# Attention projections by seven block products instead of eight, with the block sums on GpSimd and VectorE

## Chip, core and metric

One core of a Trainium2 chip runs the whole program. The metric is the device time of one execution in microseconds (us); the times shown are of separate runs, and beside them stands one execution recorded by the hardware profiler. Engines: PE is TensorE (matrix products; PEld its weight loads), DVE is VectorE, ACT is ScalarE, POOL is GpSimd, SP is the engine that issues most DMA transfers. On-chip memory is SBUF (128 partitions); matrix products are written to PSUM, which has eight banks. All data here are fp32.

## The reference, cut to what matters

1250 nodes with 768 features pass through two graph-attention layers, then through a transformer block: multi-head attention with 12 heads of 64, and a mixture of experts (8 experts, 2 per token). Only the attention's projections are changed:

```python
def _attention(x, Wqkv, Wproj):
    B, T, D = x.shape                      # 1, 1250, 768
    qkv = (x @ Wqkv).reshape(B, T, 3, H, HD)
    q, k, v = (qkv[:, :, 0], qkv[:, :, 1], qkv[:, :, 2])
    scores = jnp.einsum('bqhd,bkhd->bhqk', q, k) * jnp.float32(HD) ** (-0.5)
    attn = jax.nn.softmax(scores, axis=-1)
    out = jnp.einsum('bhqk,bkhd->bqhd', attn, v).reshape(B, T, D)
    return out @ Wproj
```

## The kernel before, in words

The input of attention is `yT`: the normalized rows, transposed, 128 partitions x 6 chunks of features (`DC`) x 1250 nodes. It is filled tile by tile (ten tiles of 125 nodes, `NT`) by the second graph layer: aggregation matmuls `pagg` (L524), layernorm on VectorE (L120 to L134), six transposes `ptr` on PE (L141) and six activations on ScalarE that write `yT` (L147).

Attention works on two heads at a time (`p`, six pairs) and on a third of the queries at a time (`CHUNKS`, 417 or 416 columns), so there are 18 units (`class Unit`). A unit's scores are computed while the unit before it is being finished. For each of ten key tiles, `scores` multiplies keys by queries into `st`, ScalarE copies `st` to `sT` (L679) and VectorE keeps a running maximum `most` (L685). Then `top` transposes `most` (`ptop`, L692), VectorE reduces it to `m` (L694), `row` spreads `m` over partitions into the PSUM tile `mb` (L701), `weights` subtracts it (L706, VectorE), takes the exponential (L707, ScalarE) and adds up the weights (`acc`, L712, GpSimd), and `values` multiplies by the values (`pav`, L720). `divide` of the unit before sums `acc` over partitions on PE (`pz`, L729) and divides on VectorE (L735, L736), writing `aT`.

Queries and keys of a pair of heads come from `queries_keys` (L639), a generator: each `yield` ends one step, and `go` runs steps at chosen places inside the three units of the pair before. Its steps are single matmuls: 2 and 4 in a unit's head, around `top` and `divide`, and three times 2 in the loop over key tiles. Keys are written to a PSUM tile with the tag of `mb` and queries to one with the tag of `pz`; ScalarE moves them out (L642). The values come from `value_rows` (L655), per tile of 125 nodes 12 matmuls into a pair of banks from `pair_psum`, moved out by ScalarE (L658).

What sets the order: inside `manual_schedule` PE runs exactly in the written order. The other engines' instructions are ordered by the framework's list scheduler when the program is built; each engine's queue then runs strictly in that order, and semaphores make one engine wait for another. A pool of tiles that takes memory of an earlier pool waits for all of that pool; with `reuse_waits="tile"` it waits only for the tiles that lay there. With `bufs=1` a tile waits until its predecessor under the same tag has been read.

From the program as it is built: `pagg` has PSUM banks 0 to 3 and `ptr` banks 4 to 6; in attention `pair_psum` has banks 0 to 3, the tag `mb` banks 4 and 5, `pz` bank 6, `pav` bank 7. In SBUF `cnt`, the graph's edge counts, lies where `aT` lies later.

Of the kernel before, what the change touches and what calls it, by code (L numbers as in the profile page):

```python
# [10 lines left out]
F32 = mybir.dt.float32  # L11
# [16 lines left out]
def gnn_ffn_kernel(  # L28
# [569 lines left out]
                transpose_rows(gpt, y, affine(yT, t, 0))  # L598


    attn = late.enter_context(tc.tile_pool(name="attn", bufs=1))
    aT = attn.tile([P, DC, N], F32, name="aT")
    with tc.tile_pool(name="att", bufs=2) as ap, \
            tc.tile_pool(name="aps", bufs=2, space=PSUM) as aps, \
            tc.tile_pool(name="apm", bufs=1, space=PSUM) as apm, \
            tc.tile_pool(name="apa", bufs=1, space=PSUM) as apa:
        heads = [slice(i * HD, (i + 1) * HD) for i in range(2)]
        BW = 105
        NB = 4
# [3 lines left out]
            return aps.tile([P, 2, 512], F32, tag="s", name=name)  # L613


        zero = ap.tile([P, RW], F32, name="zero", bufs=1)
        nc.gpsimd.memset(zero, 0.0)  # L617
        nc.gpsimd.memset(zero[:, D:D + 1], float(NOWHERE))
        for e in range(NE):
# [1 line left out]
                                zero[:, None, :].to_broadcast([P, REG // P, RW]))  # L621
        nc.gpsimd.dma_start(xd[NOWHERE:NOWHERE + P, :], zero)

        def queries_keys(p):

            wqk = ap.tile([P, DC, 2, P], F32, tag="wqk", name="wqk", bufs=1)
            for i in (1, 0):
                nc.sync.dma_start(wqk[:, :, i, :], Wqkv[:, i * D + p * P:i * D + (p + 1) * P].rearrange(
                    "(c p) f -> p c f", p=P))
            qk = ap.tile([P, 2, N], F32, tag="qk", name="qk")  # L630
            yield qk
            for c0, w in CHUNKS:
                for i in (1, 0):
                    if i == 1:
                        pq = apm.tile([P, 2, 512], F32, tag="mb", name="pk")[:, 0, :]
                    else:
                        pq = apa.tile([P, 512], F32, tag="pz", name="pq")
                    for c in range(DC):
                        nc.tensor.matmul(pq[:, :w], wqk[:, c, i, :], yT[:, c, c0:c0 + w],  # L639
                                         start=(c == 0), stop=(c == DC - 1))  # L640
                        if c == DC - 1:
                            nc.scalar.mul(qk[:, i, c0:c0 + w], pq[:, :w], 1.0 if i == 1 else HD ** -0.5)  # L642
                        yield None

        def go(steps, n):
            for _ in range(n if steps is not None else 0):
# [1 line left out]

        v = big.tile([T, NT, D], F32, tag="B", name="v")

        def value_rows(t):
            pv = pair_psum("pv")
            for s in range(2):
                for c in range(DC):
                    nc.tensor.matmul(pv[:T, s, :DH], yT[:, c, t * T:(t + 1) * T],  # L655
                                     wv[:, c, s * DH:(s + 1) * DH],
                                     start=(c == 0), stop=(c == DC - 1))
            nc.scalar.copy(v[:, t, :].rearrange("p (s d) -> p s d", s=2), pv[:T, :, :DH])  # L658

        onesf = ap.tile([T, HD], F32, name="onesf", bufs=1)  # L660
        nc.vector.memset(onesf, 1.0)

        class Unit:


            def __init__(self, p, k, qk):
                self.p, self.qk = p, qk
                self.c0, self.w = CHUNKS[k]
                self.starts = [min(b * BW, self.w - BW) for b in range(NB)]
                self.s = []  # L670

            def scores(self, j):
                w = self.w
                st = pair_psum("st")
                for i, r in enumerate(heads):
                    nc.tensor.matmul(st[:T, i, :w], self.qk[r, 1, j * T:(j + 1) * T],  # L676
                                     self.qk[r, 0, self.c0:self.c0 + w], start=True, stop=True)
                s = ap.tile([T, 2, CW], F32, tag="sT", name="sT", bufs=15)
                nc.scalar.copy(s[:, :, :w], st[:T, :, :w])  # L679
                self.s.append(s)  # L680
                if j == 1:
                    self.most = ap.tile([T, 2, CW], F32, tag="most", name="most")
                if j > 0:
                    prev = self.s[0] if j == 1 else self.most
                    nc.vector.tensor_tensor(self.most[:, :, :w], prev[:, :, :w], st[:T, :, :w], ALU.max)  # L685
# [18 lines left out]
            def weights(self, j):  # L704
                w, s = self.w, self.s[j]
                nc.vector.tensor_tensor(s[:, :, :w], s[:, :, :w], self.mb[:T, :, :w], ALU.subtract)  # L706
                nc.scalar.activation(s[:, :, :w], s[:, :, :w], AF.Exp)  # L707
                if j == 1:
                    self.acc = ap.tile([T, 2, CW], F32, tag="acc", name="acc")
                if 0 < j < self.ns:  # L710
                    prev = self.s[0] if j == 1 else self.acc
                    nc.gpsimd.tensor_tensor(self.acc[:, :, :w], prev[:, :, :w], s[:, :, :w], ALU.add)  # L712
# [22 lines left out]
                nc.vector.reciprocal(rz[:, :w], self.pz[:, :w])  # L735
                nc.vector.tensor_tensor(aT[:, self.p, self.c0:self.c0 + w], self.pav[:, :w], rz[:, :w], ALU.mult)  # L736

        steps = queries_keys(0)
        qks = [next(steps)]
        wp = load_big_weight(Wproj, "wp")  # L740
        BEFORE = 2
        with tc.manual_schedule(engines={mybir.EngineType.PE}):
            for t in range(BEFORE):
                value_rows(t)
            for _ in steps:
                pass
            u = Unit(0, 0, qks[0])
            for j in range(NT):
                u.scores(j)
                if j + BEFORE < NT:  # L750
                    value_rows(j + BEFORE)
        units = [(p, k) for p in range(DC) for k in range(NCK)]
        steps = last = None
        for n, (p, k) in enumerate(units):
            if k == 0:
                steps = None
                if p + 1 < DC:
                    steps = queries_keys(p + 1)
                    qks.append(next(steps))
            nxt = Unit(*units[n + 1], qks[units[n + 1][0]]) if n + 1 < len(units) else None  # L760
            u.ns = NT if nxt is not None else NS
            with tc.manual_schedule(engines={mybir.EngineType.PE}):

                go(steps, 2)
                u.top()
                if last is not None:
                    last.divide()
                go(steps, DC - 2)
                if nxt is not None:
                    nxt.scores(0)  # L770
                u.row()
                u.weights(0)
                u.weights(1)
                for j in range(0, NT, 2):
                    for i in range(2):
                        if nxt is not None and j + i > 0:
                            nxt.scores(j + i)
                    if j < 6:
                        go(steps, 2)
                    for i in range(2):  # L780
                        if j + i + 2 < NT:
                            u.weights(j + i + 2)
                    for i in range(2):
                        u.values(j + i)
            last, u = u, nxt
# [306 lines left out]
```

## Time and profile before

| | |
|---|---|
| median of 3 runs | 1527.41 us (1524.62 to 1529.33) |
| profiled execution | 1522.34 us, span 1520.5 us |
| granted PE clock over the span | 0.963 |
| PE busy | 1433.7 us (94%) |
| DVE busy | 811.9 us (53%) |
| ACT busy | 595.6 us (39%) |
| POOL busy | 418.6 us (28%) |
| values (`pv`, L655) | 240 matmul instructions, 79.9 us busy |
| queries and keys (`pq`, `pk`, L639) | 432 matmul instructions, 172.1 us busy |

How to read the lines that follow: a timeline line has the start in us from the beginning of the span, the length in us, engine, source line, operation, output<-inputs with their shapes, the count of merged instructions, and in brackets how long the engine stood idle before it and what released it. A group line has busy time and mean length (ns) of one. The page's section 2 cuts the span into 40 slices of 38 us; each digit is a busy share in tenths. Values and the first queries and keys are computed from about 555 to 670 us, the units run from about 670 to 1160.

### The profile page before, as it was taken

To read this page: it belongs to the slowest core of one execution; us is meant where nothing else is said; L and a number is where in the kernel's file an instruction comes from. 1 tells how busy PE (TensorE), PEld (TensorE's weight loads), DVE (VectorE), ACT (ScalarE), POOL (GpSimd) and SP (SyncE) were. 2 spreads that over 40 slices of the span, in tenths; PEclk is the share of its full clock that TensorE was granted. 3 is DMA by queue.
4 is the path that set the end of the run, shared out by engine and by line. 5 is a ranking of instruction groups with operands and counts; after the bars stand their busy time and mean duration, and the time that the engine had idled before them with its cause. 6 is when DMAs were issued, how large, how long until landed. Compare 5 with 4: busy or idle time off the path is not lost.

```text
span 1520.5 us, 15858 instructions
## 1 busy us (share of the span) xinstructions
PE 1433.7 (94%) x5952; PEld 779.0 (51%) x5952; DVE 811.9 (53%) x1311; ACT 595.6 (39%) x924; POOL 418.6 (28%) x276
## 2 busy tenths in 40 slices
PE   6787999999999999999999999999989996899997
PEld 4574555556555555543343343344333664565654
DVE  6688456434036640127778778778787764111111
ACT  4221513205116521136556646646656354221211
POOL 5000000000000010006646646655657222122222
PEclk9758999999999999999999999999999997899999
DMA  7000020010021139920000000000120432855643
GB/s 207 22 2 11 11 73 0 0 32 1 15 88 45 57 100 396 407 86 0 22 1 0 22 1 21 1 22 0 28 75 1 144 119 107 300 172 185 219 153 134
DMA packets 48199, 124.66 MB, mean 82 GB/s; under 512 B 5629, under 2 KB 22207, under 8 KB 48120
## 3 DMA queue, kind: packets, MB, share of 16 engines
q1 hardware_dynamic: 31468, 57.36, 11.5%
q0 software_dynamic: 11968, 56.26, 9.8%
q10 hardware_dynamic: 4684, 9.99, 2.2%
q8 instruction: 48, 0.79, 0.2%
q14 instruction: 31, 0.25, 0.1%
HBM read 70.47 MB, written 57.60 MB: 84 GB/s over the span
## 4 chain that ended last, share of the span: by engine, by line
PE 67%; DVE 9%; issue 7%; ACT 4%; DMA 4%; POOL 1%; POOLq 0%; SPq 0%; ACTq 0%; DVEq 0%
PE pagg L524 13%; PE st L676 8%; PE ph L204 7%; PE pav L720 7%; PE pk L639 5%; PE pv L655 5%; PE phe L1006 5%; PE poe L1015 5%; PE pq L639 4%; DMA xd<-yn,slot 2%; DVE sT L706 2%; PE po L864 2%; ACT sT L679 1%; DVE most L685 1%; PE mb L701 1%
## 5 line engine op out<-in xcount | busy, mean ns | idle before, releaser
L712 POOL TENSOR_TENSOR acc<-acc,sT 125x834 f32<-125x834 f32 (+1 forms) x139 | 273.1, 1964 | 10.9
L524 PE MATMUL pagg<-h,wt 125*125 125x385 f32 (+1 forms) x800 | 263.5, 486 | 0.4 <-DVE wt L517 0.4
L685 DVE TENSOR_TENSOR most<-most,st 125x834 f32<-125x834 f32 (+1 forms) x144 | 147.0, 1021 | 105.5 <-ACT sT L679 102.6
L524 PEld LDWEIGHTS pagg<-h,wt 125*125 125x125 f32 x800 | 147.0, 187 | 104.7 <-DVE wt L517 3.5
L706 DVE TENSOR_TENSOR sT<-sT,mb 125x834 f32<-125x834 f32 (+1 forms) x180 | 174.1, 1015 | 22.6 <-PE mb L701 22.6
L707 ACT ACTIVATE sT<-sT 125x834 f32<-125x834 f32 (+1 forms) x180 | 158.4, 900 | 49.2 <-DVE sT L706 48.8
L679 ACT COPY sT<-st 125x834 f32<-125x834 f32 (+1 forms) x180 | 151.6, 848 | 52.4 <-PE st L676 50.7
L676 PE MATMUL st<-qk 64*125 64x417 f32 (+1 forms) x720 | 164.5, 556 | 3.9 <-DVE most L685 3.8
L720 PE MATMUL pav<-sT,v 125*64 125x417 f32 (+1 forms) x720 | 151.0, 532 | 9.0 <-ACT sT L707 9.0
L617 POOL MEMSET zero<- 128x772 f32 x1 | 0.7, 742 | 530.2 <-PE ptr L141 530.2
L712 POOL TENSOR_TENSOR acc<-sT 125x834 f32<-125x834 f32 (+1 forms) x18 | 35.4, 1965 | 274.6 <-ACT sT L707 274.6
L676 PEld LDWEIGHTS st<-qk 64*125 64x125 f32 x720 | 56.5, 184 | 99.1 <-issue 42.7
L720 PEld LDWEIGHTS pav<-sT,v 125*64 125x64 f32 x720 | 42.5, 136 | 105.7 <-issue 43.9
L1015 PE MATMUL poe<-we,hT 128*128 128x384 f32 x264 | 88.8, 486 | 0.0
L639 PE MATMUL pq<-yT,wqk 128*128 128x417 f32 (+1 forms) x216 | 88.1, 534 | 0.0
L864 PE MATMUL po<-wp,aT 128*125 128x384 f32 x240 | 87.5, 498 | 0.0
L1019 DVE SCALAR_TENSOR_TENSOR sofar<-poe,weight,sofar 128x768 f32<-128x768 f32 x25 | 25.4, 1018 | 114.6 <-PE poe L1015 107.7
L1006 PE MATMUL phe<-xT,we 128*128 128x384 f32 (+1 forms) x288 | 86.6, 460 | 0.0
L639 PE MATMUL pk<-yT,wqk 128*128 128x417 f32 (+1 forms) x216 | 84.0, 526 | 0.0
L204 PE MATMUL ph<-gw,xnT 128*125 128x384 f32 x240 | 81.4, 498 | 0.5 <-DMA gw<-in_L_gnn_W_dram 0.5
L655 PE MATMUL pv<-wv,yT 128*125 128x384 f32 x240 | 79.9, 490 | 1.4 <-issue 1.4
L528 DVE RECIPROCAL rz<-pagg 125x1 f32<-125x1 f32 x20 | 3.3, 166 | 141.5 <-PE pagg L524 141.5
(222 smaller groups left out, 1788.2 us busy)
## 6 DMA issues: line engine op xcount, KB each, us to landing
xd<-zero POOLq DMA_DIRECT2D x8, 3860.0 KB, 15.2
we<-in_L_ffn_W_dram SPq DMA_DIRECT2D x16, 1152.0 KB
xr<-xd SPq DMA_DIRECT2D x25, 386.0 KB
gw<-in_L_gnn_W_dram SPq DMA_DIRECT2D x2, 2304.0 KB
wqk<-in_L_ffn_Wqkv_dram SPq DMA_DIRECT2D x12, 384.0 KB
xres<-in_x_dram SPq DMA_DIRECT2D x10, 375.0 KB
xsd<-xres ACTq DMA_DIRECT2D x10, 375.0 KB
xn<-in_x_dram SPq DMA_DIRECT2D x9, 336.0 KB
```

Source lines behind the costliest of these rows:

```text
L204: nc.tensor.matmul(po[:, s, :DH], xT[:, c, t * T:(t + 1) * T], w[:, c, s * DH:(s + 1) * DH], start=(c == 0), stop=(c == DC - 1))
L524: nc.tensor.matmul(po[:, s, :DH + s], ws[j][:, (d - d0) * T:(d - d0 + 1) * T], h[:, j, s * DH:(s + 1) * DH + s], start=(j == 0), stop=(j = ...
L639: nc.tensor.matmul(pq[:, :w], wqk[:, c, i, :], yT[:, c, c0:c0 + w], start=(c == 0), stop=(c == DC - 1))
L676: nc.tensor.matmul(st[:T, i, :w], self.qk[r, 1, j * T:(j + 1) * T], self.qk[r, 0, self.c0:self.c0 + w], start=True, stop=True)
L679: nc.scalar.copy(s[:, :, :w], st[:T, :, :w])
L685: nc.vector.tensor_tensor(self.most[:, :, :w], prev[:, :, :w], st[:T, :, :w], ALU.max)
L706: nc.vector.tensor_tensor(s[:, :, :w], s[:, :, :w], self.mb[:T, :, :w], ALU.subtract)
L707: nc.scalar.activation(s[:, :, :w], s[:, :, :w], AF.Exp)
L712: nc.gpsimd.tensor_tensor(self.acc[:, :, :w], prev[:, :, :w], s[:, :, :w], ALU.add)
L720: nc.tensor.matmul(self.pav[r, :w], v[:, j, hd0:hd0 + HD], s[:, i, :w], start=(j == 0), stop=(j == NT - 1))
L1006: nc.tensor.matmul(ph[:, :n * P], w1[:, c, f * P:(f + 1) * P], xT[:, c, :n * P], start=(c == 0), stop=(c == DC - 1))
L1015: nc.tensor.matmul(po[:, d, :DH], hT[:, f, s * P:(s + 1) * P], w2[:, f, d * DH:(d + 1) * DH], start=(f == 0), stop=(f == FC - 1))
```

## The change

A product of two matrices cut into quarters takes eight products of quarters, or seven if sums and differences of quarters are multiplied (the Strassen-Winograd form). The change uses seven for the values and for queries and keys.

- `left_sums` makes four sums of quarters of the weights and `right_sums` four of `yT`, all on GpSimd; some overwrite quarters in place, others go to `aT`, which is still unused then (`spare`), and to the tiles `t2`, `t3`, `t4`.
- `seven` runs the products, each three matmuls long. Product 1 is copied out by ScalarE; the others are added to earlier partial sums by VectorE, straight from PSUM (seven adds for six products). Products go to the banks of `mb` (`m`, `n`), `pz` (`z`) and `pav` (`v`).
- Values: the products pair tile `t` with tile `t + 5`, 384 columns wide. Queries and keys: both come from the same seven products (weights' columns: keys, queries; nodes: first half, second half), in two pieces of 313 and 312 columns. A step of `queries_keys` is now a whole product; `go` runs one before `top`, one after `divide` and three in the loop.
- The queries' scale moves into the exponential. `wp` is loaded in the last pair of heads, since its memory now holds copies of `t2` and `t3` (`kept`) till then. The scores' 15 buffers become 15 tags, `most` and `acc` get one buffer each, and the pools of attention use `reuse_waits="tile"`.

```diff
-    attn = late.enter_context(tc.tile_pool(name="attn", bufs=1))
+    attn = late.enter_context(tc.tile_pool(name="attn", bufs=1, reuse_waits="tile"))
...
-    with tc.tile_pool(name="att", bufs=2) as ap, \
+    with tc.tile_pool(name="att", bufs=2, reuse_waits="tile") as ap, \
...
-        zero = ap.tile([P, RW], F32, name="zero", bufs=1)
+        spare = aT.rearrange("p c n -> p (c n)")
+        zero = spare[:, 4 * N:4 * N + RW]
...
+        def left_sums(a, w, flat):
+            s1, s2, s4 = parts(flat, w, 3)
+            a11, a12, a21, a22 = (a[:, c:c + KH, f:f + w] for f in (0, w) for c in (0, KH))
+            nc.gpsimd.tensor_tensor(s1, a21, a22, ALU.add)
+            nc.gpsimd.tensor_tensor(s2, s1, a11, ALU.subtract)
+            nc.gpsimd.tensor_tensor(s4, a12, s2, ALU.subtract)
+            nc.gpsimd.tensor_tensor(a21, a11, a21, ALU.subtract)
+            return [a11, a12, s4, a22, s1, s2, a21]
...
+        def right(t2, t3):
+            return [y11, y21, y22, t4, y12, t2, t3]
+        def right_sums(t, t2, t3):
+            q = slice(t * T, (t + 1) * T)
+            nc.gpsimd.tensor_tensor(t3[:, :, q], y22[:, :, q], y12[:, :, q], ALU.subtract)
+            nc.gpsimd.tensor_tensor(y12[:, :, q], y12[:, :, q], y11[:, :, q], ALU.subtract)
+            nc.gpsimd.tensor_tensor(t2[:, :, q], y22[:, :, q], y12[:, :, q], ALU.subtract)
+            nc.gpsimd.tensor_tensor(t4[:, :, q], y21[:, :, q], t2[:, :, q], ALU.subtract)
+
+        FREE = ["1m", "6n", "2z", "7v", "5m", "4n", "3z"]
+        BOUND = ["1m", "6n", "7z", "4z", "2z", "5m", "3n", "1z", "6z", "7z", "4m", "2n", "5z", "3z"]
+
+        def seven(order, operands, np_, w, o11, o12, o21, o22):
...
+            for i, name in order:
+                if name == "m":
+                    two = apm.tile([P, 2, 512], F32, tag="mb", name="mq")
+                if name in "mn":
+                    b = two[:np_, "mn".index(name), :w]
+                else:
+                    b = apa.tile([P, 512], F32, tag={"z": "pz", "v": "pav"}[name], name="q")[:np_, :w]
+                for c in range(KH):
+                    lhs, rhs = operands(int(i) - 1, c)
+                    nc.tensor.matmul(b, lhs, rhs, start=(c == 0), stop=(c == KH - 1))
+                if i == "5":
+                    u4 = part(1)
+                if i == "1":
+                    nc.scalar.copy(p1, b)
+                for o, u in {"2": [(o11, p1)], "6": [(u2, p1)], "7": [(u3, u2)], "4": [(o21, u3)],
+                             "5": [(u4, u2), (o22, u3)], "3": [(o12, u4)]}.get(i, []):
+                    nc.vector.tensor_tensor(o, b, u, ALU.add)
+                yield None
...
-                nc.scalar.activation(s[:, :, :w], s[:, :, :w], AF.Exp)
+                nc.scalar.activation(s[:, :, :w], s[:, :, :w], AF.Exp, scale=HD ** -0.5)
...
+            ws = left_sums(wv, DH, spare)
+            for t in range(NU):
+                right_sums(t, t2, t3)
+            steps = queries_keys(0, right(t2, t3), True)
...
+            kept = wpool.tile([P, DC, D], F32, tag="w", name="kept").rearrange("p c d -> p (c d)")
+            ys = right(*parts(kept, NH, 2))
+            nc.gpsimd.tensor_copy(ys[5], t2)
+            nc.gpsimd.tensor_copy(ys[6], t3)
...
-                go(steps, 2)
+                go(steps, 1)
                 u.top()
                 if last is not None:
                     last.divide()
-                go(steps, DC - 2)
+                go(steps, 1)
...
                     if j < 6:
-                        go(steps, 2)
+                        go(steps, 1)
```

## The prediction

> **What bounds the kernel now.** I read the engine totals and the 40 slices first, then the groups of instructions (for the prices), then the timeline of one unit of attention, of the units that have no projection in them, and of the passage from the second graph layer into attention.
>
> ```profile
> PE 1433.7 (94%) x5952; PEld 779.0 (51%) x5952; DVE 811.9 (53%) x1311; ACT 595.6 (39%) x924; POOL 418.6 (28%) x276
> ...
> PE   6787999999999999999999999999989996899997
> ...
> DVE  6688456434036640127778778778787764111111
> ```
>
> TensorE (PE) is near full from the fourth slice on, which by itself promises a gain for every matmul taken out. But VectorE (DVE) stands at 7 to 8 all through attention (slices 18 to 30). How near to the bound that is shows in units with and without projection matmuls. In the timeline of PE, the maxima's transposes (`ptop`) mark a unit's start:
>
> ```profile
> 759.78 1.02 PE L692 MATMUL ptop<-ident,most 125*105 125x125 f32 x8
> ...
> 788.72 1.02 PE L692 MATMUL ptop<-ident,most 125*105 125x125 f32 x8
> ```
> ```profile
> 1106.10 1.10 PE L692 MATMUL ptop<-ident,most 125*105 125x125 f32 x8 [0.72 <-DVE most L685]
> ...
> 1131.82 1.10 PE L692 MATMUL ptop<-ident,most 125*105 125x125 f32 x8 [0.52 <-DVE most L685]
> ```
>
> A unit with projection takes 28.94 us, one without 25.72. The 24 matmul instructions of 0.350 us (8.4 us) that the first has and the second lacks cost only 3.2 us: just under them lies a chain of VectorE and ScalarE. The same unit on VectorE:
>
> ```profile
> 760.84 1.20 DVE L694 TENSOR_REDUCE m<-ptop 105x8 f32<-105x1000 f32 x1 [1.83 <-PE ptop L692]
> 761.95 2.75 DVE L735 RECIPROCAL rz<-pz 128x416 f32<-128x416 f32 x1
> 764.74 0.59 DVE L736 TENSOR_TENSOR aT<-pav,rz 128x416 f32<-128x416 f32 x1
> 766.70 2.89 DVE L706 TENSOR_TENSOR sT<-sT,mb 125x834 f32<-125x834 f32 x3 [1.37 <-PE mb L701]
> ...
> 778.84 1.02 DVE L685 TENSOR_TENSOR most<-most,st 125x834 f32<-125x834 f32 x1
> 780.31 1.02 DVE L685 TENSOR_TENSOR most<-most,st 125x834 f32<-125x834 f32 x1 [0.45 <-ACT sT L679]
> ```
>
> Reduce, reciprocal and multiplication follow without a gap up to 765.33; PE's transposes `mb` begin at 765.48, and from 766.70 to 779.86 VectorE has no gap. PE and VectorE are nearly even here.
>
> **Matmuls taken out, up to the first unit.** Each fp32 matmul stands in the trace as two instructions. Values: 240 become 5 pairs x 7 products x 3 x 2 = 210; 30 of them in a row took 9.84 us (from 562.47, 0.328 each): **-9.8**. First queries and keys: 72 of 417 columns at 0.350 (12 from 576.35 to 580.55) become 84 of 313. A 128-column one took 0.116 (36 `phe` in 4.18); on the line between, 313 columns take 0.266: 22.3 for 25.2, **-2.9**. VectorE adds 35 sums of 384 columns and 14 of 313 here. Price: 834 columns took 1.016 (L706), 417 took 0.591 (L736), so by the line through both 313 take 0.485 and 384 take 0.557, each under a product of 1.6 to 2.0 us, on an engine that is 0 to 2 tenths busy in these slices. Costed at nothing: the next product in the same bank comes at least two products later. Without that cover it would wait for the sum.
>
> **The passage.** Here the tail of the graph layer was filled:
>
> ```profile
> 555.51 6.04 PE L655 MATMUL pv<-wv,yT 128*125 128x384 f32 x18 [1.36 <-issue]
> ...
> 561.80 0.83 PE L141 MATMUL ptr<-ident,y 125*128 125x125 f32 x6 [0.25 <-DVE y L134]
> 562.35 2.19 ACT L147 ACTIVATE yT<-ptr,lnp 128x125 f32<-128x125 f32 x6 [1.61 <-PE ptr L141]
> ...
> 562.47 2.75 PE L655 MATMUL pv<-wv,yT 128*125 128x384 f32 x8
> 562.71 0.98 SPq L628 DMA_DIRECT2D wqk<-in_L_ffn_Wqkv_dram  x2
> ...
> 562.75 0.74 POOL L617 MEMSET zero<- 128x772 f32 x1 [530.17 <-PE ptr L141]
> ```
>
> The value rows could start at 555.51 because `pair_psum` has the banks of `pagg`, read by then. The new products write `mb`, `pz` and `pav`; these have the banks of the transposes `ptr`, which ScalarE reads until 564.54. The first of the seven waits for that, and behind it on PE, which runs this block in written order, every other product and the scores. By 564.6 the kernel before had done 18 value instructions and 6.6 more, 24.6 x 0.328: **+8.1**. The gap (554.2 to 561.8) also costs clock. Before L720 at 1112.96 PE stood idle 2.07 us; the window after it, whose last three numbers are granted clock, DMA share and GB/s:
>
> ```profile
> 1113.00:1117.00 4.00, 3.94 (x12) 1.14 (x14) 4.00 (x5) 2.56 (x3) 2.51 (x2) 0.57 0.08 25
> ```
>
> Eight `pav` took 3.08 us there where others took 1.62, the next eight `st` 2.02 for 1.67: 1.8 lost, **+1.8**. The last six transposes come after that gap; at half clock six took 1.51 (1276.94) instead of 0.83: **+0.7**.
>
> GpSimd's sums go by its row of 834 columns, 1.965: in proportion or with the slope between 834 and 832 columns (4 ns), 2.7 for each of the four of `wv` (1152 columns), 0.9 to 1.1 for each of 20 of `yT` (375), 31 in all. Tile-wise reuse lets them start when `cnt`, which lay where `aT` will, was last read (521.5, L517); with nine DMA issues of `xd` ahead (7.7 of issue, 7.8 of wait) they end near 569, but the first value products need only the first eight (near 554): hidden, by the last aggregations and then by 14 us of value products. If that cover is gone, see the third rival. The load of `wqk` can leave SP earlier than 562.71; that of `wp` moves past those of `wqk`, to the last pair of heads, some 75 us before its use: nothing. Two copies into `kept` (at most 4.4 each by the sums' rate) begin when product 4 has read `wv`; the first lies under products 3, 1 and the transposes (2.0 + 1.7 + 0.95 = 4.6), the second is needed 6 us later: nothing.
>
> A rule of the Trainium skill speaks against sums there. VectorE's maxima took 1,024 ns with GpSimd idle (600 to 672) and 1,020 with it busy (742 to 758), but those, like the new adds, have one operand in PSUM. "SBUF — State Buffer", section "SBUF: two separate sides", says that GpSimd and a VectorE instruction with two SBUF inputs or in a two-port mode lock each other out for a whole instruction; the last layernorm has such ones (L589, L134 twice), so by the rule the sum would be 1 to 3 us higher. No row shows it.
>
> **The fifteen units with projection.** A step is now one product, six instructions of 0.266 = 1.60, with 0.1 to 0.2 for the change of operands (four of 0.350 took 1.50 from 758.28, 1.60 from 767.42). A unit's head on PE, from 758.28 to `mb` at 765.48, shrinks from 7.20 to 6.20 (first step 1.70 for 1.50, second 1.80 for 3.00, transposes, row sums and first scores 2.70 as before). In the loop 8 steps of 1.80 replace 9 of 1.60 per three units: no gain. So PE offers 1.0 per unit, all of it ahead of `mb`. VectorE gets 14 adds per three units, 2.26 us per unit. Three of them (products 5 and 4 in a first step) fall into its wait for `ptop` (1.83): free. Three (6, 3 and 2 in a second step) must be done before `mb` takes the same bank. Such an add queues behind reciprocal and multiplication, which are ready first: 7.05 + 0.20 (`ptop` later) + 0.485 + 0.1 (signal, as from `mb` to L706) = 7.8 for 7.20, **+0.6**; behind it wait PE's `mb`, then all subtractions and exponentials. Ahead of the multiplication it would cost 0, ahead of the reciprocal +0.9. The loop's 8 adds (1.3 per unit) enter the stretch without gaps; scores wait on maxima there, but the last subtractions (776.04) ran some 6 us ahead of the `pav` that need them (785.66), so they can give way: +0.1, of 0 to 1.3. I take **+0.7 x 15 = +10.5**, ends -1.0 and +2.2 (-15 and +33).
>
> **GpSimd in the heads.**
>
> ```profile
> 782.57 6.05 POOL L712 TENSOR_TENSOR acc<-acc,sT 125x834 f32<-125x834 f32 x3
> ```
> Its chain of sums ends at 788.62, 1.4 after the unit's start at 787.21; PE's row sums `pz` use it at 789.66: slack 1.04, and 0.20 more with the longer first step. Four weight sums (384 columns, 1.0 each) are new per pair of heads. Behind the chain the two that product 6 needs end at 1.4 + 2.0 = 3.4, in time for it (3.5). Inside the chain they delay `pz` by 4.0 - 1.2 = 2.8. Four such heads, 0 to 11; I take 1.0 each, near the lower end, since a part can run in GpSimd's idle 10.6 us before the chain: **+4**.
>
> **Sum.** -12.7 + 10.6 + 10.5 + 4.0 = +12.4. The profiled execution took 1522.3 (span 1520.5), which gives 1534.7. The median of the runs shown is 5.1 above it: **1540**.
>
> **Rivals.** (1) Faster: the add is issued ahead of the multiplication, or VectorE's gaps take all adds, and heads shrink with PE: -12.7 + 10.6 - 0.5 x 15 to -1.0 x 15 = -10 to -17, about 1514. It decides below +0.1 per unit with GpSimd free. For it: 2.8 us of VectorE gaps at a unit's end, and 1.37 before `mb`. Against: the reciprocal's chain, and 25.72 + 2.26 = 28.0, already near 28.94. 0.20. (2) It evens out (units +0.1, GpSimd 0): 1527. 0.15. (3) Memory is not free before the last transposes: GpSimd starts at 562.75 as before, issues 7.7, sums 10.9 + 4.0: value products begin some 22 (with the ninth DMA's wait 30) us later: 1560. The memset's wait speaks for it, the tile-wise reuse against. 0.08. (4) Every add and sum lands on the path: units +1.8, GpSimd 11: +36, 1563. 0.12. My forecast, slower by 5 to 20: 0.45. That a 313-column product saves nothing is excluded by the 0.116 row.
>
> 0.3% (4.6 us) is about what a measurement can tell. Faster 0.20, same 0.15, slower 0.65. 1517 to 1560 leaves out half of (1) and most of (4).
>
> **What would show it.** PE idle of 7 us or more before the first value product, at a granted clock near 0.5 after it; 714 `q` and `mq` instructions; units of 29.3 to 30.2 between `ptop`, with the `u2` add behind `aT` and `mb` waiting on it; `pz` waiting on `acc` in the 4th, 7th, 10th and 13th unit. Units below 28.5, or value products before 562, would prove me wrong.

## The result and the profile after

The change makes the kernel slower: 1561.01 us median of 4 runs (1557.99 to 1565.51) against 1526.01 of 4 runs of the kernel before beside them (1521.51 to 1529.33), ratio 1.0229, interval 1.0210 to 1.0247. The profiled execution took 1563.34 us, with a span of 1561.6. Engine totals and slices of the changed kernel (the last line is the granted TensorE clock):

```profile
PE 1415.8 (91%) x5994; PEld 791.7 (51%) x5994; DVE 877.4 (56%) x1430; ACT 577.1 (37%) x895; POOL 471.0 (30%) x326
...
PE   5787999999999938999999999999988997799997
...
PEclk9758999999999968999999999999999998899999
```

PE is busy 17.9 us less than before, yet the span is 41.1 longer. Two slices (546 to 624 us) show 3 and 8 tenths of PE and 6 and 8 tenths of clock, where before there were nines. So most of the loss lies between the graph layer and attention, not in the units.

Two rulers split it. From the residual add of tile 6 (L589) to the first unit's top transposition (`ptop`): 158.92 us before, 191.17 after, **+32.3**. From the first `ptop` to the last (17 units): 484.89 and 489.27, **+4.4**. Together 36.6, near the 35.0 between the medians. The forecast had -2.1 and +14.5. The ends of both rulers, before:

```profile
513.70 0.95 DVE L589 TENSOR_TENSOR xres<-xres,o 125x768 f32<-125x768 f32 x1
...
672.62 1.10 PE L692 MATMUL ptop<-ident,most 125*105 125x125 f32 x8 [0.58 <-DVE most L685]
...
1157.51 1.10 PE L692 MATMUL ptop<-ident,most 125*105 125x125 f32 x8 [0.52 <-DVE most L685]
```

and in the changed kernel:

```profile
517.14 0.95 DVE L589 TENSOR_TENSOR xres<-xres,o 125x768 f32<-125x768 f32 x1
...
708.31 1.02 PE L756 MATMUL ptop<-ident,most 125*105 125x125 f32 x8
...
1197.58 1.10 PE L756 MATMUL ptop<-ident,most 125*105 125x125 f32 x8 [0.52 <-DVE most L749]
```

The passage in the timeline of the changed kernel:

```profile
543.01 0.56 POOL L624 DMA_DIRECT2D xd<-aT  x1 [6.23 <-DMA xd<-aT]
...
543.58 2.65 POOL L641 TENSOR_TENSOR aT<-aT,wv 128x1152 f32<-128x1152 f32 x1
...
544.58 15.15 DVE L589 TENSOR_TENSOR xres<-xres,o 125x768 f32<-125x768 f32 x1
...
558.07 0.84 POOL L655 TENSOR_TENSOR t<-yT 128x375 f32<-128x375 f32 x1
...
565.13 1.48 PE L141 MATMUL ptr<-ident,y 125*128 125x125 f32 x6 [14.74 <-DVE y L134]
...
566.40 8.08 PE L524 MATMUL pagg<-h,wt 125*125 125x385 f32 x18
...
574.56 61.60 SPq L697 DMA_DIRECT2D wqk<-in_L_ffn_Wqkv_dram  x4
...
582.14 1.49 PE L141 MATMUL ptr<-ident,y 125*128 125x125 f32 x6 [7.66 <-DVE onesf L720]
...
585.28 4.20 PE L680 MATMUL mq<-wv,yT 128*125 128x384 f32 x6 [1.65 <-ACT yT L147]
...
601.52 2.17 PE L680 MATMUL mq<-wv,t 128*125 128x384 f32 x6 [1.21 <-DVE v L687]
...
608.14 0.99 POOL L640 TENSOR_TENSOR aT<-wqk 128x384 f32<-128x384 f32 x1 [22.00 <-DMA wqk<-in_L_ffn_Wqkv_dram]
...
610.95 2.91 PE L680 MATMUL mq<-t,aT 128*128 128x313 f32 x6 [3.74 <-POOL aT L641]
```

Four things. VectorE's add of tile 8, 0.96 us for other tiles, lasts 15.15 and ends (559.73) 0.8 us after a train of GpSimd sums has run dry (558.91). TensorE idles 14.74 us for it and then works at half clock: 18 `pagg` in 8.08 us, 5.99 before. The first value product comes at 585.28, after the last transposes, as the forecast said. And the weights `wqk`, issued at 574.56 (the first two of the four issues that this line merges), are there only at 608.

The waits of TensorE in the changed kernel, in columns of total us, times and longest us:

```profile
PE mb L765 <- DVE qk L687: 7.8, 10, 0.8
...
PE pz L793 <- POOL acc L776: 5.7, 5, 1.3
...
PE mq L680 <- DVE v L687: 3.9, 5, 1.2
PE mq L680 <- POOL aT L641: 3.7, 1, 3.7
...
PE mq L680 <- ACT u L684: 2.5, 4, 0.7
PE mb L765 <- DVE u L687: 2.1, 4, 0.5
```

The rows `mq <- v` and `mq <- u` (and one like them, `mq <- qk`, 1.9 in all) belong to the start: product 4 (second half of the tile `mb`) waits for VectorE's adds of product 5 (first half), product 6 for ScalarE's copy of product 1. The head of a unit, from `ptop` to `mb`, in the timeline:

```profile
736.61 1.02 PE L756 MATMUL ptop<-ident,most 125*105 125x125 f32 x8
...
738.78 2.76 DVE L799 RECIPROCAL rz<-pz 128x417 f32<-128x417 f32 x1
...
741.46 0.42 DVE L687 TENSOR_TENSOR qk<-mq,u 128x313 f32<-128x313 f32 x1
...
741.79 0.58 DVE L800 TENSOR_TENSOR aT<-pav,rz 128x417 f32<-128x417 f32 x1
...
741.93 1.12 PE L765 MATMUL mb<-ident,m 105*125 105x105 f32 x8 [0.78 <-DVE qk L687]
```

The add stands behind the reciprocal but ahead of the multiplication, and `mb` follows at 5.32 us after `ptop` (5.70 before). Most units with projection last 30.2, 29.1 and 28.6 us in turn; before, nearly all of them lasted 28.9.

### The profile page after: what moved, and what is told of

It is laid out like the page before. It is cut to its first block, busy times and chain, and to the rows that moved or that the text cites. A ratio compares the mean times of both kernels' runs of the same rounds, so it can differ in the third digit from the quotient of the medians.

```text
span 1561.6 us, 16121 instructions
## 1 busy us (share of the span) xinstructions
PE 1415.8 (91%) x5994; PEld 791.7 (51%) x5994; DVE 877.4 (56%) x1430; ACT 577.1 (37%) x895; POOL 471.0 (30%) x326
## 4 chain that ended last, share of the span: by engine, by line
PE 55%; DVE 13%; issue 9%; ACT 5%; POOL 5%; DMA 4%; POOLq 0%; ACTq 0%; SPq 0%; DVEq 0%
PE pagg L524 12%; PE ph L204 7%; PE st L739 5%; PE pav L784 5%; PE mq L680 5%; PE phe L1082 5%; PE poe L1091 4%; PE q L680 4%; POOL acc L776 4%; DVE sT L770 2%; DVE rz L799 2%; DMA xd<-yn,slot 2%; ACT sT L743 2%; ACT sT L771 2%; DVE most L749 2%
## 5 line engine op out<-in xcount | busy, mean ns | idle before, releaser
L770 DVE TENSOR_TENSOR sT<-sT,mb 125x834 f32<-125x834 f32 (+1 forms) x180 | 174.8, 1014 | 12.7 <-PE mb L765 12.7
L204 PE MATMUL ph<-gw,x1T 128*125 128x384 f32 x240 | 78.8, 489 | 0.0
L1084 ACT ACTIVATE hT<-phe 128x384 f32<-128x384 f32 (+1 forms) x27 | 12.6, 466 | 160.4 <-PE phe L1082 157.0
L1082 PEld LDWEIGHTS phe<-xT,we 128*128 128x128 f32 x288 | 52.1, 190 | 33.7
```

The lines of the kernel that those rows point to most:

```text
L204: nc.tensor.matmul(po[:, s, :DH], xT[:, c, t * T:(t + 1) * T], w[:, c, s * DH:(s + 1) * DH], start=(c == 0), stop=(c == DC - 1))
L1082: nc.tensor.matmul(ph[:, :n * P], w1[:, c, f * P:(f + 1) * P], xT[:, c, :n * P], start=(c == 0), stop=(c == DC - 1))
```

## The experiments

All ratios are to the kernel before, run beside. "Passage" is the first ruler, "units" the second, both in us of the profiled execution. The kernels that are not in the table (e1, e6, e7, e10, e12, e14, e15) were run once each.

| kernel | median | ratio, 95% interval | passage | units |
|---|---|---|---|---|
| before | 1526 | 1 | 158.9 | 484.9 |
| changed | 1561.0 | 1.0229 [1.0210, 1.0247] | 191.2 | 489.3 |
| e2 sums on VectorE | 1556.7 | 1.0194 [1.0177, 1.0211] | 187.8 | 488.8 |
| e3 zero writes partly later | 1552.1 | 1.0177 [1.0158, 1.0195] | 179.5 | 489.8 |
| e4 own banks | 1555.2 | 1.0184 [1.0167, 1.0201] | 181.5 | 490.0 |
| e5 GpSimd's order | 1559.5 | 1.0216 [1.0196, 1.0237] | 191.3 | 484.0 |
| e8 zero writes late | 1544.1 | 1.0117 [1.0090, 1.0143] | 172.5 | 489.4 |
| e9 as e8, but sums of `wv` and `yT` on VectorE | 1545.2 | 1.0130 [1.0103, 1.0157] | 171.8 | 489.3 |
| e11 all of it | 1519.5 | 0.9958 [0.9943, 0.9972] | 151.0 | 488.1 |
| e11b sums on GpSimd | 1517.6 | 0.9937 [0.9922, 0.9953] | 148.9 | 486.9 |
| e13 two value groups first | 1518.3 | 0.9941 [0.9922, 0.9960] | 148.9 | 486.1 |

**Three trains of GpSimd work in the kernel before.** My first theory: GpSimd's train of sums locks VectorE out until it ends.

```diff
+                if t == 7:                       # behind the residual add, scratch tile dum
+                    nc.gpsimd.tensor_copy(dum[:T], xr[:, :384])
+                    for i in range(18):
+                        nc.gpsimd.tensor_tensor(dum, dum, dum, ALU.subtract)
```

> The kernel before, with 18 extra GpSimd subtractions (two SBUF inputs, 384 numbers a partition, some 0.9 us each, 16 us together) that start when tile 7's residual add is done; they work on a scratch tile, and nothing waits for them. Theory of the lock (GpSimd's train of SBUF sums keeps VectorE's two-SBUF-input add out until the train has run dry): the residual add of tile 8, some 6 us after the train's start, lasts about 10 us in place of 0.96, and ends within a microsecond of the train's end; the end of the run comes 5 to 12 us later than before's. Theory of the transfer (the add of 15.15 us in the changed kernel waited for its tile of x, slowed by the early zero writes): all ten adds stay at 0.9 to 1.0 us, and the time stays within 3 us of before's.

> The same place, with 36 GpSimd copies of 192 numbers (one SBUF input) in place of the subtractions, 8 to 14 us together. If any GpSimd instruction on SBUF keeps the add out: the add of tile 8 lasts until the train's end, 3 to 8 us. If only two-input instructions do: all adds stay at 0.9 to 1.0 us. Theory of the transfer: they stay there too.

> The same place, with 12 pairs of a subtraction (0.9 us) and a GpSimd memset (0.3 us). If the lock is held by one instruction at a time, or is freed by an instruction that reads nothing: the add of tile 8 lasts at most 1 us longer than 0.96. If GpSimd keeps it as long as it has anything queued: some 9 us, to the train's end. Theory of the transfer: 0.9 to 1.0.

The add of tile 8 took 1.55, 1.12 and 0.96 us; the times were 1527.39, 1523.59 and 1523.57 beside 1524.03. The theory in this form fell. In that train each sum read what the one before had written, so I tried one without such gaps:

```diff
+                        nc.gpsimd.tensor_tensor(m[:, (i % 2) * 384:(i % 2 + 1) * 384],
+                                                m[:, 768:1152], m[:, 768:1152], ALU.subtract)
```

> The kernel before, again with 18 GpSimd subtractions of 125x384 (two SBUF inputs) after tile 7's residual add; now neighbours write two different places of a dead tile and none reads what its neighbour wrote, so each can begin as the one before it ends, where the first train's each read the one before and stood 0.06 us apart. Theory of the lock held over a train without gaps: VectorE's residual add of tile 8, or another of its SBUF-to-SBUF steps, falls into the train and lasts until its end, 5 to 10 us, and the end of the run comes 4 to 10 us later than before's. Rival (the lock passes at every instruction's end; the 15.15 us had another cause): no VectorE step is longer than its usual time by more than 1 us, and the time is within 3 us of before's.

The add took 1.07 us, and the longest GpSimd sum 1.54 in place of 0.82: the two engines took turns. The rival held; 1528.54 us, inside the usual scatter.

**The start's sums on VectorE.**

```diff
-            nc.gpsimd.tensor_tensor(...)          # left_sums(wv), right_sums, first left_sums(wqk)
+            nc.vector.tensor_tensor(...)
```

> The changed kernel with the sums of the start (of the value weights, of the LN output, of the first head pair's weights) on VectorE in place of GpSimd; the units' sums stay on GpSimd. Theory of the lock: the residual add of the last tile is back at 1 us, its transposes come 13 to 17 us earlier, and the time falls to 1545 to 1549 us, less 2 to 4 us for the half clock that follows the idle stretch, plus up to 5 us where VectorE's own 12 us of sums delay the last tiles. Theory of the transfer: the add of the last tile stays at 15 us and the time within 3 us of the changed kernel's.

Timeline of this kernel:

```profile
545.12 0.96 DVE L589 TENSOR_TENSOR xres<-xres,o 125x768 f32<-125x768 f32 x1
...
568.73 0.96 DVE L589 TENSOR_TENSOR xres<-xres,o 125x768 f32<-125x768 f32 x1 [9.32 <-DMA xres<-in_x_dram]
```

The add of tile 8 is back at 0.96 us, but that of tile 9 now waits for its load until 568.73: a second delay had been hidden behind the first. So the time fell by some 4 us, not by the 12 to 16 of the lock theory.

**The zero writes later.** In the change GpSimd issues eight of the nine writes that fill the expert buffer `xd` (31 MB) from 529 us on, 35 us earlier than before (564), and the ninth at 543.

```diff
-        (zero and the nine writes of xd ahead of left_sums(wv))
+        (the same behind the copies into kept)
```

> The changed kernel with the zero writes of the expert buffer (31 MB, GpSimd's DMA queue) issued after the copies at the start's end in place of ahead of the sums. Theory of the transfer for the add of 15.15 us: it falls to 1 us and the time by 14 to 18 us. Theory of the lock: it stays at some 15 us (GpSimd's train starts up to 14 us earlier without the wait for the writes ahead of it, so the train may lie elsewhere and the add be shorter, but it still ends with a GpSimd instruction). Theory of the late weight load: the first head pair's weights land some 10 us earlier, the wait of 3.74 us ahead of the queries' second product goes, and with it half clock of 1.8 us: 4 to 6 us less.

Only six of the nine moved: three were still issued at 535, since nothing ties a write to its place. Directly behind those three came GpSimd's sums, and now another VectorE step lasted: the scaling `y` of L134, 5.51 us for 0.67:

```profile
535.14 2.98 POOL L817 DMA_DIRECT2D xd<-aT  x3 [0.30 <-POOL aT L815]
...
539.85 5.51 DVE L134 TENSOR_SCALAR y<-xres,mv,rstd 125x768 f32<-125x768 f32 x1
```

With their source first copied from the weight sums all nine wait:

```diff
+                nc.gpsimd.tensor_copy(zero, spare[:, 5 * N:5 * N + RW])   # behind left_sums of the first wqk
                 nc.gpsimd.memset(zero, 0.0)
```

> The changed kernel with the zero writes of the expert buffer issued behind the first head pair's weight sums (their source is first written from those sums, so that they cannot be moved ahead). GpSimd's sums of the start stay. Theory (zero writes hold up the loads of x and of the first head pair's weights; the lock is a second cost of its own): the last tile's add waits for no load and the first weights are there when their products come; the first top transposition comes 8 to 14 us earlier than in the changed kernel, and the time falls to 1546 to 1553 us; steps of VectorE of 5 us or more during GpSimd's trains stay. Rival (loads are not what the end waits for): within 3 us of the changed kernel.

> As the run before in this list, and the sums of the value weights and of the LN output on VectorE, so that neither the lock nor the zero writes can act in the passage. Theory that the two together make up the lost passage: no VectorE step of 5 us, no wait of the last add for its load; TensorE's longest wait in the passage falls from 14.7 us to under 6 us; the first top transposition comes 17 to 24 us earlier than in the changed kernel, and the time is 1537 to 1544 us. Rival (VectorE's own sums, some 13 us of them, replace what they remove): 1548 us or more.

Timeline of `e8_xd_after_sums`:

```profile
535.37 2.37 POOL L644 TENSOR_TENSOR t<-yT 128x375 f32<-128x375 f32 x2
...
535.87 1.17 DVE L589 TENSOR_TENSOR xres<-xres,o 125x768 f32<-125x768 f32 x1
...
574.68 0.99 POOL L629 TENSOR_TENSOR aT<-wqk 128x384 f32<-128x384 f32 x1
```

The passage is 18.7 us shorter in e8, more than the 8 to 14 expected. The same GpSimd sums, with no write ahead of them, cost VectorE one instruction at most (adds 1.05 to 1.73, one scaling 2.60), and the weights do not come late. I had expected long steps to stay; they went with the writes. Moving the sums of `wv` and `yT` to VectorE as well (e9) brings nothing more: the intervals overlap. TensorE still stands 12.25 us ahead of the last transposes there, where I had expected less than 6: there are no products yet to fill the last tile's layernorm. The reverse, early writes alone in the kernel before (their source a dead tile of 80 partitions):

```diff
+                if t == 6:
+                    (zero in a dead tile; the nine writes of xd from here)
```

> The kernel before with nothing changed but the zero writes of the expert buffer, issued when tile 6's residual add is done (their source is a dead tile of 80 partitions), some 50 us earlier than they were. Theory of the loads: the last tile's add waits 5 to 15 us for its load of x, TensorE idles and its clock falls, and the run ends 6 to 15 us later than before's. Rival (the transfers share the engines without harm): within 3 us of before's.

1620.42 us against 1526.69, some 94 more where the theory had 6 to 15. Timeline:

```profile
572.26 0.96 DVE L592 TENSOR_TENSOR xres<-xres,o 125x768 f32<-125x768 f32 x1 [15.33 <-DMA xres<-in_x_dram]
...
666.81 5.93 PE L644 MATMUL pk<-yT,wqk 128*128 128x417 f32 x12 [74.78 <-DMA wqk<-in_L_ffn_Wqkv_dram]
```

The wait for `x` was about as expected; the 74.78 us for `wqk` I had not expected, and it is no measure of the change, where the same load came 33 us after its issue (in windows of 20 us from 520 to 640, the transfers moved 197 to 287 GB/s here; in the changed kernel 379 to 398 from 540 to 600).

**Writes and train together.** The kernel of `e10_before_early_xd` with a train of 36 sums behind the writes, once with a small copy between, once without:

```diff
                     (the nine writes of xd)
+                    nc.gpsimd.tensor_copy(one, xr[:, :192])                # only in e12; there copy and train are written behind tile 7's add
+                    for i in range(36):
+                        nc.gpsimd.tensor_tensor(dum[:T, i % 2], one, one, ALU.subtract)
```

> The kernel before with both: the zero writes of the expert buffer issued early, as in the run of before with early zero writes, and behind them on GpSimd a train of 36 subtractions (125x192, neighbours independent, some 17 us), reading a dead tile. Theory (a GpSimd train keeps VectorE out to its end only while GpSimd's own queue of DMAs is at work): VectorE's add of tile 8, or a scaling step next to it, lasts 8 to 17 us and ends with the train. Rival (the forms or places of the changed kernel's sums are what matters): every VectorE step stays within 1 us of its usual time, as in the two trains without the writes.

> The kernel before with early zero writes and the train of 36 subtractions (125x192) directly behind the last of them, with no copy between. If VectorE starves where sums follow a write of GpSimd's queue directly: its add of tile 8 or a scaling step next to it lasts 5 us or more and ends with the train. Rival: every VectorE step stays within 1 us of its usual time, as with the copy between.

Timeline of `e12_xd_and_train`, with the copy:

```profile
543.62 0.36 POOL L596 COPY most<-xres 125x192 f32<-125x192 f32 x1
...
544.06 18.10 POOL L598 TENSOR_TENSOR dum<-most 125x192 f32<-125x192 f32 x36
...
544.33 1.05 DVE L592 TENSOR_TENSOR xres<-xres,o 125x768 f32<-125x768 f32 x1 [1.40 <-DMA xres<-in_x_dram]
```

Timeline of `e15_train_next`, without it:

```profile
543.28 0.58 POOL L605 DMA_DIRECT2D xd<-most  x1 [16.86 <-DMA xd<-most]
...
543.88 16.72 POOL L608 TENSOR_TENSOR dum<-most 125x192 f32<-125x192 f32 x36
...
544.62 16.79 DVE L592 TENSOR_TENSOR xres<-xres,o 125x768 f32<-125x768 f32 x1 [1.34 <-DMA xres<-in_x_dram]
```

The times were 1626.65 and 1628.66 us. In the second, this is the add of the changed kernel, made in the kernel before: 16.79 us, ending 0.8 us after the train's end. In every run where sums stood behind a write of GpSimd's own queue (the changed kernel, e3, e4, e5, e6, e14, e15) a VectorE step from SBUF to SBUF starved to the train's end; where nothing or a copy stood ahead (e1, e7, e8, e12, and the first sums of e3) the engines took turns, and VectorE lost 2.6 us at most (a scaling of 3.27 for 0.68 in e3). A memset between did not help:

```diff
                     nc.gpsimd.dma_start(xd[NOWHERE:NOWHERE + P, :], zero)
+                    nc.gpsimd.memset(s2[:, 0, 0:1], 0.0)
                 nc.gpsimd.tensor_tensor(s2, s1, a11, ALU.subtract)
```

> The changed kernel with one GpSimd memset of a single column between the last zero write and the sums that follow it (their order among themselves shifts a little, too). If VectorE starves only where the sums follow a write of GpSimd's queue directly: its residual add of tile 8 falls from 15 us to 1 to 3 us, and the time by up to 14 us. Rival (the transfers in flight decide, not what stands between): the add, or another VectorE step from SBUF to SBUF, still lasts 8 us or more, to the end of GpSimd's train.

1565.14 us, and the add lasted 17.04:

```profile
542.67 0.12 POOL L643 MEMSET aT<- 128x1 f32 x1
...
543.60 17.04 DVE L589 TENSOR_TENSOR xres<-xres,o 125x768 f32<-125x768 f32 x1
```

That a copy ends it rests on one pair of runs; a copy in the changed kernel wasn't tried.

**One bank for each product of the start.**

```diff
-                    two = apm.tile([P, 2, 512], F32, tag="mb", name="mq")
+                    b = sp.tile([P, 512], F32, tag="o" + name, name="q")[:np_, :w]   # banks 0 to 3
```

> The changed kernel with four PSUM tiles of one bank each for the seven products of the start, in the banks that the aggregation used, and the first unit's scores in the other four. Theory of the banks: the waits of products 4 and 6 on the VectorE adds and the ScalarE copy of the other half of their tile go (8 to 10 us over seven groups of seven), and the first value product no longer waits for the transposes' banks (6 to 8 us of products ahead of the last transposes, unless GpSimd's sums hold them back): 8 to 16 us less. Rival (the adds' rate or GpSimd's sums bound the start): within 3 us of the changed kernel.

The passage fell by 9.7 us, with the waits `mq <- v`, `mq <- u` and `mq <- qk` (8.3 us in all) gone and the first product ahead of the last transposes; but then the queries' second product stood 12.66 us, waiting for sums of the late weights:

```profile
612.22 3.41 PE L683 MATMUL q<-t,aT 128*128 128x313 f32 x6 [12.66 <-POOL aT L640]
```

**GpSimd's order in the units.**

```diff
-            with tc.manual_schedule(engines={mybir.EngineType.PE}):
+            with tc.manual_schedule(engines={mybir.EngineType.PE, mybir.EngineType.Pool}):
                 ...
+                if k == NCK - 1 and p + 2 < DC:   # the next pair's left_sums behind the chain
+                    ahead = queries_keys(p + 2, ys, False)
```

> The changed kernel with the units' GpSimd instructions in a fixed order: the four sums of a head pair's weights behind the accumulation chain of the unit before in place of inside it. Theory of GpSimd's order: the four waits of 1.3 us of the softmax sums for the accumulation go, and the time falls by 5 us, less up to 4 times 1 us where the second product of the next pair now waits for its sums. Rival (the chain's end is set elsewhere): within 2 us of the changed kernel.

The units took 484.0 us, 5.3 less; the four units of 30.2 went to 29.1, which is 4.6 of it. The ratio's interval overlaps that of the changed kernel, so this rests on the ruler (which moved by up to 0.7 us in five runs that left the units alone, and by 2.4 in e14) and on the waits. Those of this kernel:

```profile
PE pz L793 <- POOL acc L776: 0.6, 2, 0.3
```

**Small adds in the units.**

```diff
-                    nc.vector.tensor_tensor(o, b, u, ALU.add)
+                    z = w if free else 8
+                    nc.vector.tensor_tensor(o[:, :z], b[:, :z], u[:, :z], ALU.add)
```

> The changed kernel; in the units (not in the start) each VectorE add of a seven works on 8 columns in place of 312 or 313, so queries and keys of the later head pairs come out wrong; their tiles are zeroed once by GpSimd in the start. Theory of the forecast (0.7 us a unit for adds on the path): the 18 units take 489 - 10 = 479 us. Theory that the adds lie in slack of VectorE and of the banks' order: the stretch from the first to the last top transposition stays at 487 to 490 us.

The units took 483.8 us: 5.4 less, about half of what the forecast's theory gave and more than its rival allowed; each of the first 14 is 0.2 to 0.4 us shorter. Waits of this kernel:

```profile
PE mb L768 <- DVE qk L688: 4.7, 10, 0.5
...
PE mb L768 <- DVE u L688: 0.8, 4, 0.2
```

Their sum is 5.5 us; in the changed kernel it was 7.8 + 2.1 = 9.9. Even an add of 8 columns waits behind the reciprocal.

**All together.** `e11_all` joins e4, e5 and e9; in `e11b_all_pool` the start's sums stay on GpSimd; `e13_two_rows` puts two groups of value rows first.

> The changed kernel with all that helped: zero writes behind the first weight sums, the start's other sums on VectorE, one bank for each product of the start, GpSimd's order fixed in the units. If the parts add up: 1545 (writes and VectorE sums) less 5 (order) less 8 to 11 (banks, and products ahead of the last transposes) = 1529 to 1532 us, 0.2 to 0.4% above before. Rival (the parts overlap: one idle stretch was counted twice): 1536 us or more.

> As the run before, but the start's sums stay on GpSimd. If, with the zero writes out of the way, it does not matter which of the two engines makes them: within 2 us of the run before. If VectorE's adds and sums get into each other's way there: 2 to 5 us less.

> As the run before (sums on GpSimd), and two groups of value rows, 14 products, ahead of the first queries and keys, in place of one. If TensorE's idle time at the last tile's layer norm still costs: the second group gives the late weights of queries and keys time and the sums of the last tile's rows too; 1 to 4 us less. Rival: within 1 us of it.

All three are faster than the kernel before, by 0.4 to 0.6%, and among themselves not to be told apart: which engine makes the start's sums, and a second group of value rows, changed nothing that could be measured. The parts gave more than their sum: with late writes, own banks are worth 23.6 us of passage (e8 to e11b; the fixed order alone left the passage at 191.3), not 9.7. Timeline of `e11b_all_pool`:

```profile
562.32 2.17 PE L672 MATMUL q<-wv,yT 128*125 128x384 f32 x6 [1.36 <-issue]
...
569.38 0.83 PE L141 MATMUL ptr<-ident,y 125*128 125x125 f32 x6 [1.01 <-DVE onesf L712]
```

TensorE now has products to run while the last tile is normalized, waits 1.01 us instead of 7.66, and keeps its full clock (0.83 for six transposes, not 1.49).

## Why the prediction was wrong

The direction was right; 1561 lies 21 us over the forecast and 1 over the range. Point by point:

- **Matmuls taken out, -12.7: borne out, nearly in full.** With the new waits removed, the passage of e11b is 10.0 us shorter than before (148.9 for 158.9).
- **The passage, +10.6: the wait named was there, but it was not the large one.** The value products did wait for the transposes' banks, and the half clock came. The measured passage is +32.3, where the forecast's terms gave -2.1. From the kernel before to e11b, on to e8 and to the changed kernel it goes by -10.0, +23.6 and +18.7. Four steps failed, which the next four points name.
- **"With nine DMA issues of `xd` ahead (7.7 of issue, 7.8 of wait)"**: I priced the writes as time on GpSimd's queue and never asked where 31 MB go. Issued 35 us earlier, they shared the DMA engines with the loads of `x` and `wqk`. This and the next step are worth 18.7 us (e8). The writes are the root of both: with the sums on VectorE, later writes took 16.0 us off the passage (e2 to e9); with the writes late, moving the sums took off 0.6 (e8 to e9).
- **"Hidden, by the last aggregations"**: GpSimd's sums were hidden, but their effect on VectorE was not. The rule I weighed (the Trainium skill, "SBUF — State Buffer", section "SBUF: two separate sides": the one that starts first keeps the other out for a whole instruction) agrees with e7 and e8, where an add or a scaling lost up to 1.9 us. It does not give the 15.15, 17.04 and 16.79 us, which are whole trains: the step said to be "1 to 3 us higher" by the rule, and left out of the sum, was some 14 there.
- **"Costed at nothing: the next product in the same bank comes at least two products later"**: true of banks 4 and 5, but the program's waits go by tile, and `m` and `n` are halves of one tile. Product 4 comes directly after product 5 and waits for its adds. Measured: 8.3 us of waits, and together with the wait for the transposes' banks, which the forecast had at 10.6, 9.7 (e4) to 23.6 us (e8 to e11b).
- **"The load of `wqk` can leave SP earlier ...: nothing"**: it did leave just after the last aggregation, but that ended at 574.48 now (554.16 before). So the load left at 574.56, 11.9 us later than before, and landed 33 us later among the zero writes. TensorE waited 3.74 us for it and went on at half clock.
- **The units' adds, +10.5: mis-sized.** Nothing of it came: the 17 units took 4.4 us more than before, and 5.3 of that is GpSimd's (e5). The adds are not free: on 8 columns in place of 313 the units took 5.4 less (e6). But the add went ahead of the multiplication, the case that I had priced at 0, not behind it. `mb` waits for the add as named, 14 times, 0.7 us each, but comes no later than before (5.32 us after `ptop`, 5.70 before); that the shorter heads paid for the adds is inferred from this.
- **GpSimd in the heads, +4.0: right.** Four waits of 1.3 us in the units named; e5 took 4.6 us off these four units, 5.3 off all.

Of the rivals, the two at 1560 and 1563 came near by number, not by cause: GpSimd did start early, and the units did not pay. Of the signs, the 714 instructions, the idle time at half clock and the `pz` waits came true; units of 29.3 or more came where GpSimd's sums stood in the chain, four of 30.2, and once behind such a unit (29.4). Two units, of 28.3 and 28.45 us, lay below the 28.5 that I had named as a sign against me. The direction did not hang on the zero writes: without them (e8) the kernel is still 1.2% slower, mostly by bank waits larger than the forecast's. Without those and with GpSimd's order fixed (e11b) it is 0.6% faster.

## What to carry to other kernels

When a change moves a step earlier on a queue, follow its bytes, not only its issue: a bulk write that was harmless behind the last load is costly in front of it. Work put under another stage has to be checked for what it shares with that stage (DMA engines, SBUF access, a PSUM tile), since there are no rows of that in the profile before. And remove suspects together as well as singly: late writes, banks and order took 16.9, 5.8 and 1.5 us off the median singly (the last not clear of the noise) and 43.4 together. At two places the runs show why: what was removed alone uncovered the next wait (9.32 us for `x` in e2, 12.66 for the sums of `wqk` in e4).

## What the runs showed of the hardware

- Sums on GpSimd behind a DMA that its own queue issued, directly or with a one-column memset between, kept VectorE's SBUF-to-SBUF step out for the whole train: 15.15, 17.04 and 16.79 us for 0.96, 5.51 for 0.67. The same sums without it took turns with VectorE (adds of 1.05 to 1.73 us, single scalings of 2.60 and 3.27). Why the write matters is open.
- Here the writes of GpSimd's software queue crowded out small loads. DMA view of the changed kernel from 574 to 608 us:

```profile
q0 software_dynamic: 2062, 12.43, 91.2%
q1 hardware_dynamic: 1568, 0.79, 7.8%
```

  The columns are packets, MB and share of 16 engines: 0.79 MB of weights took 33 us among packets of 6 KB; in e9, without the writes, 5 us. The Trainium skill, "DMA: Bandwidth & Descriptors", section "Queues, rings and completion order", says that an engine goes round its queues packet by packet. An estimate from that and the view: 98 weight packets per engine, each behind one of 6 KB at 25 GB/s (12.43 MB in 91.2% of 34 us, on 16 engines), take some 26 us of the 33. It takes the view's packets for those of the page, which no run shows.
